# More copied groups, and single rows of table A fetched by SyncE, in a graph network layer on one Trainium2 core

## The chip, the cores and the metric

The kernel runs on one core of a Trainium2 chip. The time is the device time of the program in microseconds, as a median over runs. The engines are TensorE (PE in the profile, its weight loads PEld), VectorE (DVE), ScalarE (ACT), GpSimd (POOL) and SyncE (SP, which only issues transfers and loads registers).

## The reference

A graph network layer over 12,500 nodes of 64 features and 200,000 edges of 32 features, the edges sorted by destination. Everything is float32.

```python
msg_in = concatenate([nodes[row], nodes[col], edge_features], axis=-1)   # row = source, col = destination
messages = relu(msg_in @ mW1 + mb1) @ mW2 + mb2                          # hidden width 128
aggregated = segment_sum(messages, col, num_segments=12500)
upd_in = concatenate([nodes, aggregated], axis=-1)
x = layernorm(x + relu(upd_in @ uW1 + ub1) @ uW2 + ub2)
```

## The kernel before

The first layer's product is split in three: a node's share as a source is table A (`x @ mW1[:64]`, 12,500 rows of 128 floats in HBM), its share as a destination is table B, and the edge's own features are multiplied in place. Tables A and B are written by the kernel at the start.

The edges go in 1563 tiles of 128. Six tiles are a group, or step (`SUB`, 261 steps), two steps are a super (`SUP` = 12 tiles). For step `s`:

- `gather(s)` lets POOL issue one indirect transfer for each tile: 128 rows of table A, one for each edge's source, land in the `xg` buffer of the step (L220; the first ten steps gather rows of `x` instead). Nine buffers (`ROWB`) let POOL run ahead, and `frees` says after which step a buffer is free again.
- `windows(s + 2)` lets SP read the step's window numbers into registers (L285) and fetch 32 rows of table B for each tile or for several tiles with the same window (L293, later one transfer for each tile, L291).
- `select(g + 1)` (DVE, L254 and L260) compares destinations with window slots, and `load(g + 1)` (SP, L273) then fetches the edge features into the same operand; `loadd(g + 2)` (SP, L236) fetches destinations for the super after.
- `edge_part(s)` (PE, L384) multiplies the operand with the window rows and edge weights. `node_part(s)` adds the gathered rows (DVE, L410) and takes the relu (ACT, L411). `collect(s)` (PE, L443) sums the messages by destination.
- `update` and what follows it run once for some 400 nodes each and write the output (`store`, SP, L533).

In a *copied* group (`COPIED`) POOL gathers four tiles only. For the last two, x lies in SBUF column by column (`xtop`, `xbot`); the 128 columns of the edges' sources are copied one by one into `xc`, 64 by ACT (`singly`, L355) and 64 by DVE (`joined`, L362), from addresses that are loaded from `col_a` into registers, and PE multiplies `xc` with the weights (L387). The add is then L407 and the relu L408. `PACE` gives how many groups a step's copying advances, so how often a group is copied: 105 of 261.

The order of the program is written out by hand, step by step, and each engine runs its instructions in that order. Within step `s` SP has `windows(s + 2)`, in even steps `load(g + 1)`, in odd steps `loadd(g + 2)`, and now and then a store or a chunk of table B. A transfer of SP waits for the one that was issued eight before it.

Of the kernel before, what the change touches and what calls it, by code (L numbers as in the profile page):

```python
# [10 lines left out]
F32 = mybir.dt.float32  # L11
I32 = mybir.dt.int32
AF = mybir.ActivationFunctionType
ALU = mybir.AluOpType
AX = mybir.AxisListType
ET = mybir.EngineType

P = 128
N, D, DE, DH = 12500, 64, 32, 128
# [5 lines left out]
SUB = 6  # L25
# [4 lines left out]
NSUB = -(-NT // SUB)  # L30
# [39 lines left out]
XBASE = 8320  # L70
U8 = mybir.dt.uint8
YBASE = XBASE + 4 * XCOLS
LEAD = 8
PACE = ((11, 0.42), (50, 0.446), (130, 0.429), (261, 0))
FINAL = 258


# [5 lines left out]
COPIED = []  # L83
for s in range(NSUB):
    while progress(s) >= len(COPIED) + 1 and s + 3 < FINAL:
        COPIED.append(s + 3)
LAST = 4 * (N - 1)
ACTS, CHUNK = 64, 8

# [23 lines left out]
def gnn_kernel(ctx: ExitStack, tc: tile.TileContext, x1T, x, eT, e_rows, src, src_row, dst, dst_row, wlist, wrow, wnext, whalf,  # L113
# [24 lines left out]
    nc = tc.nc  # L138
# [4 lines left out]
    A = dram.tile([NPAD, DH], F32, name="tab_a")  # L143
# [11 lines left out]
    col_a = const.tile([P, 2, P, 2], I32, name="col_a")  # L155
# [47 lines left out]
    def tiles(s):  # L203
        return range(s * SUB, min((s + 1) * SUB, NT))

    def gathered_tiles(s):
        return tiles(s)[:SUB - 2 * (s in COPIED)]

    def gather(s):

# [14 lines left out]
    with tc.tile_pool(name="sup", bufs=2) as sup, tc.tile_pool(name="work", bufs=2) as work, tc.manual_schedule():  # L225
# [131 lines left out]
        def joined(s, part, of):  # L357

            todo = [(o, k, ACTS + e) for o, k, lo, hi in portion(s, P - ACTS) for e in range(lo, hi, 2)]
            for o, k, a, m in share(todo, part, of):  # L360
                for e, top, bot in addresses(k, a, m, ET.DVE):
                    nc.vector.tensor_tensor(o[:, e:e + 1].bitcast(I32), top.bitcast(I32), bot.bitcast(I32),  # L362
                                            op=ALU.bitwise_or)

        xc = {}

        def parts(n):

            if n == SUB:
                return [(slice(0, 2), SUB // 2)]  # L370
            return [(slice(b, b + 1), (n - b + 1) // 2) for b in range(2) if n > b]
# [18 lines left out]
        def node_part(s):  # L390

            n = len(tiles(s))
            pc = pcs.pop(s)
            h = work.tile([P, 2, SUB // 2, DH], F32, name="h")
            if s < XG:
                xt = xs.pop(s)
                for i in range(n):
                    k, b = divmod(i, 2)
                    q = 64 * b
                    nc.tensor.matmul(pc[:, b, k, :], xt[q:q + 64, k, :], w1a[q:q + 64], start=False,  # L400
                                     stop=i + 2 >= n)
                nc.scalar.activation(h, pc, AF.Relu)
            else:
                a = xg.pop(s)[0].rearrange("p (b k) f -> p b k f", b=2)
                if s in COPIED:
                    m = SUB // 2 - 1
                    nc.vector.tensor_tensor(pc[:, :, :m], pc[:, :, :m], a[:, :, :m], op=ALU.add)  # L407
                    nc.scalar.activation(h, pc, AF.Relu)  # L408
                for b, m in parts(n) if s not in COPIED else []:
                    nc.vector.tensor_tensor(h[:, b, :m], pc[:, b, :m], a[:, b, :m], op=ALU.add)  # L410
                    nc.scalar.activation(h[:, b, :m], h[:, b, :m], AF.Relu)  # L411
            hs[s] = h
# [270 lines left out]
        def rest(s):  # L683

            if 3 <= s < 9 and s % 2:
                others((s - 3) // 2 * 4, (s - 3) // 2 * 4 + 4)
            if 3 <= s < 11:
                zeros(s - 3, 8)
            if s == 6:
                first_nodes(8, NODES)  # L690
            if s == 9:
                columns_list()
            if s == 1:
                relative(8 * SUP, 8 * SUP + WCH)
            elif s == 2:
                relative(8 * SUP + WCH, NT)
                halves(4 * SUP, NTP // 2)
            elif s == BS:
                nc.sync.dma_start(wa, wrow.rearrange("o (p c) -> (o p) c", c=NSUP))
                nc.sync.dma_start(wb, wnext.rearrange("o (p c) -> (o p) c", c=NSUP))  # L700
                nc.scalar.dma_start(w2, mW2)
                nc.scalar.dma_start(u1a, uW1[D:2 * D, :])
                nc.scalar.dma_start(b2c, mb2.rearrange("(f o) -> f o", o=1))
                nc.vector.memset(uz[:D], 0.0)
                nc.vector.memset(ux[:D], 0.0)
                nc.vector.memset(eps, EPS)
                nc.vector.memset(ones, 1.0)
                nc.vector.tensor_copy(ux[D:], ident[D:, D:])
                nc.scalar.dma_start(uz[D:], uW1[0:D, :])
                nc.scalar.dma_start(ux[ONE:ONE + 1], ub2.rearrange("(o f) -> o f", o=1))  # L710
                nc.scalar.dma_start(ub1_s, ub1.rearrange("(f o) -> f o", o=1))
                nc.scalar.dma_start(u2, uW2)
            elif s == BS + 2:
                weights()
                checks()
# [54 lines left out]
        n = UPD[K - 1]  # L770
# [8 lines left out]
        for s in range(last + 2):  # L779
            g, j = divmod(s, SUP // SUB)  # L780
            while gathered < NSUB and frees(gathered) < s:
                gather(gathered)
                gathered += 1
            tail = due.get(s - 1) == K - 1

            def earlier(n):

                return next((u for d, u in due.items() if u + 2 < K and s - d == n and (n < 2 or u + 3 < K)), None)
            if tail:
                norm(K - 1)  # L790
            if s + 2 < NSUB:
                windows(s + 2)
            if s < NSUB:
                node_part(s)
                joined(s, 0, 3 if j == 0 and g + 1 < NSUP else 2)
            if s in at_end:
                for stage, u in at_end[s]:
                    stage(u)
            for stage, n in ((squares, 2), (statistics, 3), (deviation, 4)):
                if earlier(n) is not None:  # L800
                    stage(earlier(n))
            if 1 <= s <= NSUB:
                collect(s - 1)
            if s + 1 in due:
                close(due[s + 1])
            if j == 0 and g + 1 < NSUP:
                select(g + 1, s)
                load(g + 1)
                counts(g + 1)
            if j == 1 and g + 2 < NSUP:  # L810
                loadd(g + 2)
            if chunks and s >= BS and chunks[0] < NCH + NB * (s + 1 - BS) / (SUP // SUB * (GE - 1) - BS):
                chunk_b(chunks.pop(0), [Bv])
            if s in due and due[s] + 1 < K:
                carry(due[s] + 1)
            if s in due and due[s] + 2 != K:
                update(due[s])
            if s + 1 < NSUB:
                if s + 1 < XG:
                    transpose(s + 1)  # L820
                edge_part(s + 1)
            if earlier(4) is not None:
                norm(earlier(4))
            if earlier(1) is not None:
                residual(earlier(1))
            if s == UPD[K - 1]:
                update(K - 2)
            if s == UPD[K - 1] + 1:
                residual(K - 2)
            if due.get(s) == K - 1:  # L830
                activated(K - 1)
                residual(K - 1)
                squares(K - 1)
                statistics(K - 1)
                deviation(K - 1)
            if s + 2 in due and due[s + 2] + 1 < K:
                columns(due[s + 2])
            if s == UPD[K - 1]:
                columns(K - 1)
            rest(s)  # L840
            joined(s, 2 if j == 0 and g + 1 < NSUP else 1, 3 if j == 0 and g + 1 < NSUP else 2)
            singly(s, 0, 1)
            if s in due and due[s] + 2 < K:
                activated(due[s])
            if s == UPD[K - 1]:
                activated(K - 2)
            if tail:
                store(K - 1)
            if earlier(4) is not None:
                store(earlier(4))  # L850
# [3 lines left out]
                          skip_runtime_bounds_check_because="a count of edges")  # L854
    with tc.If(flag > 0), tc.tile_pool(name="gen", bufs=1) as up:
# [25 lines left out]
        first = up.tile([P, 1], F32, name="first")  # L881
        nc.vector.tensor_scalar(first, spare, -1.0, float(NPAD + P), op0=ALU.mult, op1=ALU.add)

        with tc.For_i(0, NT, 1) as t:
# [26 lines left out]
            pc = psum.tile([P, DH], F32, name="pcg", tag="pc")  # L911
# [4 lines left out]
            h = up.tile([P, DH], F32, name="hg")  # L916
# [6 lines left out]
            m = up.tile([P, 1], F32, name="m")  # L923
# [22 lines left out]
        with tc.For_i(0, NB, 1) as c:  # L946
# [24 lines left out]
            o = up.tile([P, D], F32, name="o")  # L971
# [49 lines left out]
```

## Time and profile before

| | |
|---|---|
| Time, median of 3 runs | 1716.34 us (1715.81 to 1716.83) |
| Profiled execution, its own time | 1714.18 us |
| Its span | 1712.3 us |
| Mean granted TensorE clock | 0.585 |
| Busy: PE, DVE, ACT, POOL | 1456.2, 1053.3, 1537.2, 1279.5 us |
| Bytes moved | 191.23 MB, 112 GB/s in the mean |

A line of a group gives the source line, the engine, the operation, the tiles written and read, the count, then the busy time in all, the nanoseconds of one, and the idle time of the engine just before them with what ended it. A line of the waits gives who waited for whom, the total in us, how often, and the longest. SP has no busy share: its instructions appear with their durations (least, median, most, in ns) where one source line is asked for, and its waits where they are asked for by engine. "issue" is idle time in which the engine waited for nothing that the profile shows.

### The profile page before, as it was taken

To read this page: it belongs to the slowest core of one execution; us is meant where nothing else is said; L and a number is where in the kernel's file an instruction comes from. 1 tells how busy PE (TensorE), PEld (TensorE's weight loads), DVE (VectorE), ACT (ScalarE), POOL (GpSimd) and SP (SyncE) were. 2 spreads that over 40 slices of the span, in tenths; PEclk is the share of its full clock that TensorE was granted. 3 is DMA by queue.
4 is the path that set the end of the run, shared out by engine and by line. 5 is a ranking of instruction groups with operands and counts; after the bars stand their busy time and mean duration, and the time that the engine had idled before them with its cause. 6 is when DMAs were issued, how large, how long until landed. Compare 5 with 4: busy or idle time off the path is not lost. (4 is left out here: it accounts for less than half of the span.)

```text
span 1712.3 us, 46949 instructions
## 1 busy us (share of the span) xinstructions
PE 1456.2 (85%) x9604; PEld 1251.9 (73%) x9604; DVE 1053.3 (62%) x7476; ACT 1537.2 (90%) x7151; POOL 1279.5 (75%) x1362
## 2 busy tenths in 40 slices
PE   2696889897888888898889999898878898999998
PEld 2585778776777786887777777776667677777776
DVE  1426666666666666666666666666666666666662
ACT  0277999999999999999999999999999999999982
POOL 7777777777777777777777777777777777777774
PEclk8675555555555555555555555556665656565666
DMA  8783434433333333333334343333333333443342
GB/s 209 207 180 100 119 109 127 117 104 89 98 93 101 95 100 97 99 103 100 104 101 110 106 113 103 106 110 103 106 103 109 111 107 108 113 112 105 105 113 76
DMA packets 205949, 191.23 MB, mean 112 GB/s; under 512 B 56129, under 2 KB 172053, under 8 KB 205669
## 3 DMA queue, kind: packets, MB, share of 16 engines
q1 hardware_dynamic: 147828, 92.48, 19.6%
q0 software_dynamic: 43296, 86.79, 18.6%
q10 hardware_dynamic: 14546, 8.93, 1.9%
q8 instruction: 91, 1.49, 0.4%
q14 instruction: 188, 1.54, 0.3%
HBM read 170.55 MB, written 17.50 MB: 110 GB/s over the span
## 5 line engine op out<-in xcount | busy, mean ns | idle before, releaser
L220 POOL DMA_INDIRECT xg<-tab_a,src_s x1293 | 1221.1, 944 | 394.2 <-issue 357.6
L355 ACT ACTIVATE xc<-xtop,xbot 128x1 f32 x6720 | 1274.5, 288 | 32.9 <-issue 22.9
L362 DVE TENSOR_TENSOR xc<-xtop,xbot 128x1 int32 x6720 | 575.0, 154 | 442.2 <-issue 429.5
L443 PE MATMUL sums<-sel,h 128*128 128x32 f32 x3126 | 643.3, 373 | 83.0 <-ACT h L408 42.5
L443 PEld LDWEIGHTS sums<-sel,h 128*128 128x128 f32 x3126 | 609.5, 296 | 108.0 <-ACT h L408 48.2
L384 PE MATMUL pc<-rhs,l 64*128 64x128 f32 x3126 | 418.7, 413 | 59.3 <-DMA l<-in_eT 15.2
L384 PEld LDWEIGHTS pc<-rhs,l 64*128 64x128 f32 x3126 | 348.8, 293 | 119.4 <-issue 62.8
L410 DVE TENSOR_TENSOR h<-pc,xg 128x768 f32<-128x768 f32 x147 | 139.5, 949 | 57.5 <-PE pc L384 27.8
L411 ACT ACTIVATE h<-h 128x768 f32<-128x768 f32 x147 | 122.3, 833 | 27.6 <-DVE h L410 26.8
L254 DVE TENSOR_TENSOR l<-l,cps 128x768 f32<-128x768 int32 (+1 forms) x134 | 126.7, 946 | 29.3 <-DMA l<-in_dst_row 17.4
L440 PEld LDWEIGHTS <-one 128*1 128x1 bf16 x1563 | 56.9, 83 | 89.3 <-issue 80.3
L440 PE MATMUL cnt<-sel,one 128*1 128x32 bf16 x1563 | 92.6, 187 | 0.5 <-issue 0.3
L408 ACT ACTIVATE h<-pc 128x768 f32<-128x768 f32 x105 | 83.8, 798 | 7.8 <-DVE pc L407 7.4
L407 DVE TENSOR_TENSOR pc<-pc,xg 128x512 f32<-128x512 f32 x105 | 73.4, 699 | 27.9 <-PE pc L387 23.8
L387 PE MATMUL pc<-w1a,xc 64*128 64x128 f32 x420 | 81.2, 388 | 0.0
L260 DVE TENSOR_TENSOR sel<-cps,drc 128x384 f32<-128x384 f32 x131 | 71.4, 545 | 12.0 <-PE sums L443 12.0
L387 PEld LDWEIGHTS pc<-w1a,xc 64*128 64x128 f32 x420 | 72.1, 301 | 0.0
L220 POOL DMA_INDIRECT xg<-in_x,src_s x60 | 57.4, 957 | 19.1 <-issue 17.7
L494 PE MATMUL cps<-ux,xw 128*128 128x64 f32 x252 | 45.9, 341 | 20.0 <-DVE sel L260 17.4
L480 PE MATMUL pu<-xw,uz 128*128 128x480 f32 (+1 forms) x64 | 61.2, 1059 | 0.0
L598 ACT COPY tb<-pb 128x512 f32<-128x512 f32 (+1 forms) x13 | 7.4, 570 | 58.7 <-DMA tab_a<-tb 26.8
L494 PEld LDWEIGHTS cps<-ux,xw 128*128 128x128 f32 x252 | 41.1, 247 | 25.4 <-DVE sel L260 19.6
(105 smaller groups left out, 691.6 us busy)
## 6 DMA issues: line engine op xcount, KB each, us to landing
l<-in_dst_row SPq DMA_DIRECT2D x262, 96.0 KB
l<-in_eT SPq DMA_DIRECT2D x262, 96.0 KB
xg<-tab_a,src_s POOLq DMA_INDIRECT x1293
rhs<-tab_b SPq DMA_DIRECT2D x361, 32.0 KB
tab_b<-tb SPq DMA_DIRECT2D x13, 512.0 KB
rhs<-tab_b SPq DMA_DIRECT2D x387, 16.0 KB
tab_a<-tb ACTq DMA_DIRECT2D x12, 512.0 KB
out<-y SPq DMA_DIRECT2D x31, 128.0 KB
```

Source lines behind the costliest of these rows:

```text
L220: nc.gpsimd.indirect_dma_start(out=a[:, i, :] if s < XG else a[:, i // 2, i % 2, :], out_offset=None, in_=A[:, :] if s >= XG else x[:, :], ...
L254: nc.vector.tensor_tensor(l[r], l[r].bitcast(I32), node[r].unsqueeze(2).broadcast_to([r.stop - r.start, SUP // 2, P]), op=ALU.is_equal)
L355: nc.scalar.activation(o[:, e:e + 1], top.bitcast(F32), AF.Identity, bias=bot.bitcast(F32))
L362: nc.vector.tensor_tensor(o[:, e:e + 1].bitcast(I32), top.bitcast(I32), bot.bitcast(I32), op=ALU.bitwise_or)
L384: nc.tensor.matmul(pc[:, b, k, :], L[g][q:q + 64, m, :], rhs[g % 2][q:q + 64, w, :], start=s >= XG or k == 0, stop=s >= XG and not copied)
L387: nc.tensor.matmul(pc[:, b, k, :], xc[s][q:q + 64], w1a[q:q + 64], start=False, stop=True)
L408: nc.scalar.activation(h, pc, AF.Relu)
L410: nc.vector.tensor_tensor(h[:, b, :m], pc[:, b, :m], a[:, b, :m], op=ALU.add)
L411: nc.scalar.activation(h[:, b, :m], h[:, b, :m], AF.Relu)
L440: nc.tensor.matmul(pn[:, bass.ds(ws[i], WIN)], one, SB[g][:, k0 + i, :, 1], start=False, stop=ends and i == n - 1)
L443: nc.tensor.matmul(ps[:, bass.ds(ws[i], WIN)], h[:, i % 2, i // 2, :], S[g][:, k0 + i, :], start=False, stop=ends and i == n - 1)
L494: nc.tensor.matmul(py[:, i], xw[u % 2][:, i * P:(i + 1) * P], ux, start=i == 0, stop=False)
```

## The change

`PACE` rises in its three stretches, so that 107 groups are copied. A second list, `SINGLE`, holds four groups (51, 97, 162 and 245) that are not copied, and in which POOL gathers four tiles only, too. The 256 rows of table A that the last two tiles need are fetched by SP, one row of 512 B in one transfer, into `xr`. `ROWPACE` gives the edges a step: 3.5 from step 12, 3.0 from 45, 2.3 from 90 and 1.6 from 136, two transfers an edge (one for each of the two tiles). `fetched(s)` issues a step's share at the end of the step: it loads the row numbers from `col_a` into SP's registers and issues the transfers. DVE then adds the gathered and the fetched rows in two instructions. `xr` has one buffer. In all there are 1024 such transfers in 204 steps, from step 12 to step 242.

```diff
-PACE = ((11, 0.42), (50, 0.446), (130, 0.429), (261, 0))
+PACE = ((11, 0.435), (50, 0.4565), (130, 0.4335), (261, 0))
...
+ROWPACE = ((12, 3.5), (45, 3.0), (90, 2.3), (136, 1.6))
+SINGLE, QUOTA = [], {}
+step, found = ROWPACE[0][0], 0.0
+while step < NSUB - 8:
+    done, a = 0, step
+    while done < P and step < NSUB - 8:
+        found += next(r for b, r in reversed(ROWPACE) if step >= b)
+        n = min(int(found) // 2 * 2, P - done)
+        found -= n
+        QUOTA[step] = len(SINGLE), done, done + n
+        done += n
+        step += 1
...
+    SINGLE.append(next(c for c in range(step + 1, NSUB) if c not in COPIED))
+    step = SINGLE[-1] + 1
...
-        return tiles(s)[:SUB - 2 * (s in COPIED)]
+        return tiles(s)[:SUB - 2 * (s in COPIED or s in SINGLE)]
...
+        A4 = A.rearrange("n (c d) -> (n c) d", c=4)
+
+        def fetched(s):
+
+            if s not in QUOTA or QUOTA[s][1] == QUOTA[s][2]:
+                return
+            i, lo, hi = QUOTA[s]
+            k = SINGLE[i] - LEAD
+            if lo == 0:
+                xr[SINGLE[i]] = work.tile([P, 2, DH], F32, name="xr", bufs=1)
+            o = xr[SINGLE[i]]
+            _, v = nc.values_load_multi_w_load_instructions(
+                col_a[k % P:k % P + 1, k // P].rearrange("k e b -> k (e b)")[:, 2 * lo:2 * hi], engines=[ET.SP], min_val=XBASE,
+                max_val=YBASE + LAST, skip_runtime_bounds_check_because="sources are node numbers")
+            for e in range(lo, hi):
+                for b, first in enumerate((XBASE, YBASE)):
+                    w = v[2 * (e - lo) + b].with_bounds(min_val=first, max_val=first + LAST, guaranteed_mod_val=0, out_of_modulus=4)
+                    nc.sync.dma_start(o[e:e + 1, b], A4[bass.ds(w - first, 4), :].rearrange("c d -> (c d)").unsqueeze(0))
...
+                if s in SINGLE:
+                    m = SUB // 2 - 1
+                    nc.vector.tensor_tensor(h[:, :, :m], pc[:, :, :m], a[:, :, :m], op=ALU.add)
+                    nc.vector.tensor_tensor(h[:, :, m], pc[:, :, m], xr[s], op=ALU.add)
+                    nc.scalar.activation(h, h, AF.Relu)
...
             rest(s)
+            fetched(s)
             joined(s, 2 if j == 0 and g + 1 < NSUP else 1, 3 if j == 0 and g + 1 < NSUP else 2)
             singly(s, 0, 1)
```

More of the change, by code (lines that the diff above doesn't have):

```diff
@@ L86 @@
         COPIED.append(s + 3)
+ROWPACE = ((12, 3.5), (45, 3.0), (90, 2.3), (136, 1.6))
[10 more added lines that the diff above has]
+        step += 1
+    if done < P:
+        QUOTA = {k: v for k, v in QUOTA.items() if k < a}
+        break
+    SINGLE.append(next(c for c in range(step + 1, NSUB) if c not in COPIED))
+    step = SINGLE[-1] + 1
 LAST = 4 * (N - 1)
@@ L365, in gnn_kernel @@
         xc = {}
+        A4 = A.rearrange("n (c d) -> (n c) d", c=4)
[14 more added lines that the diff above has]
+                    nc.sync.dma_start(o[e:e + 1, b], A4[bass.ds(w - first, 4), :].rearrange("c d -> (c d)").unsqueeze(0))
+        xr = {}
         def parts(n):
@@ L408, in node_part @@
                     nc.scalar.activation(h, pc, AF.Relu)
-                for b, m in parts(n) if s not in COPIED else []:
+                if s in SINGLE:
[3 more added lines that the diff above has]
+                    nc.scalar.activation(h, h, AF.Relu)
+                for b, m in parts(n) if s not in COPIED and s not in SINGLE else []:
                     nc.vector.tensor_tensor(h[:, b, :m], pc[:, b, :m], a[:, b, :m], op=ALU.add)
```

## The prediction

> **What bounds the kernel now.** I read the page first (busy time of the engines, then the costliest groups), then busy time by stretch, then SyncE's own waits by stretch, and last what one of its transfers costs to issue.
>
> ```profile
> PE 1456.2 (85%) x9604; PEld 1251.9 (73%) x9604; DVE 1053.3 (62%) x7476; ACT 1537.2 (90%) x7151; POOL 1279.5 (75%) x1362
> ...
> L220 POOL DMA_INDIRECT xg<-tab_a,src_s x1293 | 1221.1, 944 | 394.2 <-issue 357.6
> L355 ACT ACTIVATE xc<-xtop,xbot 128x1 f32 x6720 | 1274.5, 288 | 32.9 <-issue 22.9
> L362 DVE TENSOR_TENSOR xc<-xtop,xbot 128x1 int32 x6720 | 575.0, 154 | 442.2 <-issue 429.5
> ```
>
> POOL looks 75% busy, but its idle time is "issue": it waits for nothing that the profile shows. One gather costs (1221.1 + 394.2)/1293 = 1.249 us, and 1353 of them (60 more at the start) fill the program. One copied column costs ACT (1274.5 + 32.9)/6720 = 0.195 us and DVE (575.0 + 442.2)/6720 = 0.151 us.
>
> ```profile
> core 0: us, PE busy (x) PEld busy (x) DVE busy (x) ACT busy (x) POOL busy (x), PEclk, DMA share, GB/s
> 141.00:344.00 203.00, 169.55 (x1177) 154.97 (x1177) 136.24 (x941) 187.61 (x900) 153.61 (x163) 0.53 0.41 114
> 344.00:623.00 279.00, 236.07 (x1524) 208.44 (x1526) 180.77 (x1385) 276.20 (x1337) 210.89 (x224) 0.54 0.34 96
> 623.00:907.00 284.00, 247.11 (x1564) 215.55 (x1560) 186.26 (x1413) 281.27 (x1365) 214.66 (x228) 0.54 0.36 101
> ...
> 1072.00:1339.00 267.00, 225.66 (x1485) 189.87 (x1484) 170.85 (x1249) 254.20 (x1205) 201.74 (x214) 0.60 0.38 107
> ...
> 1590.00:1712.30 122.30, 108.49 (x707) 87.35 (x706) 60.74 (x349) 79.22 (x340) 78.34 (x83) 0.65 0.35 97
> ```
>
> The stretches are the change's own: counted by the adds of L407 and L410 (one a step from step 10), 141 us is about step 13, 344 step 45, 623 step 90, 907 step 136, 1072 step 163, 1339 step 204 and 1590 step 243. From 344 to 907 ACT is busy 276.2 of 279 and 281.3 of 284 us: there the consumers of the gathers (PE, DVE, ACT) run behind POOL at ACT's pace and catch up. From 1072 on ACT has 5% to spare, and POOL sets the pace, about 6.4 us a step. So two engines are full in turn; the third, SyncE (SP), is on no busy line, and it is the one that the change loads. Its waits, in six stretches from 141, 344, 623, 907, 1072 and 1339 us in this order:
>
> ```profile
> SPq L273 <- DVE l L254: 106.9, 16, 21.1
> SPq L608 <- DVE tb L606: 26.7, 10, 5.9
> ...
> SPq L273 <- DVE l L254: 139.1, 22, 8.9
> SPq L533 <- DVE y L526: 5.5, 3, 3.6
> ...
> SPq L273 <- DVE l L254: 94.5, 22, 7.2
> SPq L533 <- DVE y L526: 6.9, 4, 3.1
> ...
> SPq L273 <- DVE l L254: 30.9, 14, 6.0
> ...
> SPq L533 <- DVE y L526: 4.2, 3, 1.9
> ...
> SPq L273 <- DVE l L254: 50.9, 19, 6.1
> ...
> SPq L533 <- DVE y L526: 2.3, 2, 1.2
> ...
> SPq L273 <- DVE l L254: 26.6, 18, 2.7
> SPq L291 <- PE pc L384: 6.3, 23, 0.4
> SPq L533 <- DVE y L526: 3.3, 5, 0.8
> SPq L291 <- PE cps L496: 2.4, 6, 0.9
> ```
>
> That is SP's free time: 134, 145, 101, 35, 53 and 30 us. It shrinks because the rows of table B come in more and more transfers (L293, then L291). I leave the short waits on PE out of it, because their releases fall within the issue of the transfer before; the last stretch has some 9 us of them in the rows shown. In its last stretch SP is free 30 of 251 us:
>
> ```profile
> 1402.23 3.93 SPq L291 DMA_DIRECT2D rhs<-tab_b  x6
> 1406.27 0.83 SPq L273 DMA_DIRECT2D l<-in_eT  x2
> 1408.12 3.09 SPq L291 DMA_DIRECT2D rhs<-tab_b  x6
> ```
>
> Six issues take 3.09 us from the first start to the last end, one after the other.
>
> **The change, part by part.** *POOL.* 105 copied groups become 107 (two gathers less each), and four groups lose two gathers each: 1353 become 1341, 12 x 1.249 = 15.0 us less, spread over the program.
>
> *ACT, DVE, PE.* Two more copied groups are 128 more columns on ACT and on DVE: 128 x 0.195 = 24.9 us and 128 x 0.151 = 19.4 us. Where ACT is full (steps 45 to 135) the rate rises by 0.015 to step 50, by 0.0105 to step 130 and by 0.0045 after, in groups of 64 ACT columns each: 61 columns, 61 x 0.195 = 12 us on the path there, 6 of them from step 90 on; before 344 us ACT has 15 us of room and after 1072 us 5%, so the rest I cost at nothing while that room lasts (13 us if it does not). PE's eight more matmuls and the second DVE add of the four groups are some 4 us in all, beside ACT's work.
>
> *SP.* 256 single rows for each of four groups: 1024 transfers, each with a register instruction, and 204 register loads. Between the stretches' borders fall 228, 260, 200, 80, 128 and 128 transfers and 33, 43, 44, 20, 32 and 32 loads. The trace has no transfer of one table row; its neighbours are:
>
> ```profile
> L291 SPq FUSED_REGOPS  x387: 37/37/43, 1271.0 to 1688.1; - x194
> ...
> L291 SPq MOVE rhs<-tab_b x387: 29/29/35, 1271.1 to 1688.2; - x194
> L291 SPq DMA_DIRECT2D rhs<-tab_b x387: 296/316/1555, 1271.2 to 1688.3; - x194
> ...
> L311 SPq DMA_DIRECT2D cols<-in_src_row x2: 275/357/439, 111.3 to 113.9; - x2
> ...
> L285 SPq TENSOR_LOAD <-wint x245: 447/720/1219, 35.5 to 1686.0; - x123
> ...
> L608 SPq DMA_DIRECT2D tab_b<-tb x14: 398/405/581, 26.2 to 354.8; - x14
> ...
> L655 SPq DMA_DIRECT2D wint<-in_wlist x1: 313/313/313, 13.7 to 13.7; - x1
> ```
>
> L291 is the same thing with 32 rows of 512 B: 316 ns, with 37 + 29 ns of register work before it. Six of them in 3.09 us are (3.09 - 0.316)/5 = 0.555 us each, of which 0.04 is a wait instruction that a fetch lacks: 0.51 us at the upper end. The lower end is the same without the transfer's own 0.316: 0.20 us. What one row costs between them is the disputed number. One row of 8 KB cost 313 ns (L655), as much as 32; but of L311's two transfers, alike but for 128 and 124 rows, the second took 275 instead of 439 ns, 0.63 times, and a count that can't be dealt out evenly is what a single row has too. I take 0.63 x 0.316 = 0.20, so 0.40 us a fetch, and 0.72 + 0.05 = 0.77 us a load (L285's median; 0.447 at the least).
>
> [...]
>
> SP's added work against its free time, at 0.40 and 0.77: 91 + 25 = 116 against 134; 104 + 33 = 137 against 145; 80 + 34 = 114 against 101; 32 + 15 = 47 against 35; 51 + 25 = 76 against 53; and 76 against 30. The first two fit. The third is over by 13, of which ACT's 6 us lengthen the steps anyway: 7. Then 12, 23 and 46. SP issues in order: behind each run of fetches stand the next windows (L291, L293) and the eT loads (L273), and PE waits for those.
>
> ```profile
> PE pc L384 <- DMA l<-in_eT: 15.2, 17, 1.8
> ```
>
> PE already waits for eT 17 times, so there is little lead to eat: one step, 6 us. After step 242 the fetches end; the last stretch held 122 us at POOL's pace with PE busy 108.5, so 14 us can be made up there. POOL's 15 us are then worth nothing: it runs ahead until its nine buffers are full.
>
> The added waits are cheap. DVE's second add waits for the group's last fetch, issued two or three steps earlier; a new group's first fetch waits for that add, one step behind it.
>
> Sum: 12 (ACT) + 7 + 12 + 23 + 46 = 100; less 6 and 14: **80 us slower**. The profiled execution took 1714.2 us, 1.9 above its span and 2.2 below the median of the runs: 1794 us, 1795 on the scale of the runs.
>
> **The rivals.** *A dearer fetch*, the same way: at 0.51 us (L291 whole) the six stretches are over by 7, 21, 29, 21, 37 and 60, 175 in all, less 20: 1869 us. For it: L655. *A cheaper one*, 0.30: ACT 12, then 4, 10 and 33, 59 less 20: 1753 us.
>
> *The fetches are hidden, and POOL's cut counts.* This is the other side. The last stretch decides: at 0.20 us a fetch and 0.52 a load (L285's least) its need is 128 x 0.20 + 32 x 0.52 = 42 us, just what its 30 us and the short waits on PE (12 with the rows not shown) hold. Then SP is never late, ACT's 12 us are made up after 1072 us, and the end comes with POOL's: 1714.2 - 15.0 = 1699 us. It decides below about 0.22 us. For it: L311's shorter issue, and rates of fetching that fall as SP's free time falls. Against it: the register work alone is 0.20.
>
> *They cancel.* Between 0.22 and 0.27 us the last stretch's overrun of 10 to 20 us eats the 15: 1711 to 1718 us, no change.
>
> *ACT becomes the bound* without SP being late: 24.9 us more on an engine busy 90%. Its room after 1072 us (267 - 254 us in one stretch alone) takes that up; it would end at 1699 to 1705 us, and counts with the second rival.
>
> **How the numbers follow.** About 0.2% (3.4 us) is what a measurement tells from no change. Slower by SP: 0.72, of which some 0.40 lie from 0.30 to 0.45 us a fetch, the rest on both sides. Hidden: 0.22. Cancelled: 0.06. The likeliest case alone spans 1735 to 1870 us. The range has to hold the hidden case as well, so 1697 to 1880 us; about 0.1 lies above (a fetch beyond 0.52 us) and a little below.
>
> **What would show it.** Right: SP's wait L273 <- DVE L254 nearly gone from 623 us on; PE's waits for eT and for the rows of table B (L384) grown to tens of microseconds from about 907 us; ACT below 95% there; POOL with gaps that end with a consumer's add and not with "issue"; the fetch line at some 0.40 us from start to start. Wrong: fetches at 0.25 us or less from start to start, SP still waiting for DVE after 1339 us, POOL unbroken to the end and a span near 1697 us. If SP is saturated from the first stretch on, the fetch is dearer than I took it.

## The result, and the profile after

| | before | after |
|---|---|---|
| Time, median of 6 runs each | 1716.59 us (1715.81 to 1717.89) | 1872.89 us (1868.43 to 1879.98) |
| Profiled execution and its span | 1714.18, 1712.3 us | 1879.98, 1878.1 us |
| Mean granted clock | 0.585 | 0.561 |

The change makes the kernel slower by 156 us: 1.0915 times (95% interval 1.0891 to 1.094). The forecast was 80 us slower. The sign and the mechanism held, the size did not.

In the kernel after, lines have moved: the gathers are L238 (before L220), ACT's copies L373 (L355), DVE's L380 (L362), the edge products L422 (L384), the adds L445 and L453 (L407 and L410), SP's eT load L291 (L273), the load of destinations L254 (L236), the select L272 (L254), the rows of table B L311 and L309 (L293 and L291), their register load L303 (L285). New are the fetch L401 and its register load L395. The page of the kernel after:

```profile
span 1878.1 us, 50490 instructions
PE 1525.9 (81%) x9612; PEld 1311.8 (70%) x9612; DVE 1069.7 (57%) x7608; ACT 1574.1 (84%) x7279; POOL 1268.8 (68%) x1350
...
L238 POOL DMA_INDIRECT xg<-tab_a,src_s x1281 | 1210.2, 945 | 533.7 <-issue 345.6
L373 ACT ACTIVATE xc<-xtop,xbot 128x1 f32 x6848 | 1298.3, 281 | 54.2 <-issue 42.5
L380 DVE TENSOR_TENSOR xc<-xtop,xbot 128x1 int32 x6848 | 585.1, 155 | 476.1 <-issue 466.5
...
L422 PE MATMUL pc<-rhs,l 64*128 64x128 f32 x3126 | 456.2, 428 | 224.9 <-DMA l<-in_eT 125.8
...
L272 DVE TENSOR_TENSOR l<-l,cps 128x768 f32<-128x768 int32 (+1 forms) x134 | 127.4, 951 | 179.4 <-DMA l<-in_dst_row 171.7
...
xr<-tab_a SPq DMA_DIRECT2D x1024, 0.5 KB
```

No engine with a busy line is full: every share went down, and POOL's gathers now have 188 us of idle time that is not "issue" (533.7 - 345.6), where before it was 37 (394.2 - 357.6). The waits of the kernel after (who waited for whom, us in total, times, longest) name what they wait for:

```profile
DVE l L272 <- DMA l<-in_dst_row: 171.7, 68, 6.8
POOL xg L238 <- DVE h L453: 126.5, 71, 5.9
PE pc L422 <- DMA l<-in_eT: 125.8, 55, 5.0
...
POOL xg L238 <- DVE pc L445: 38.1, 23, 4.5
...
PE pc L422 <- DMA rhs<-tab_b: 27.2, 29, 2.6
```

DVE and PE wait for transfers that SP issues (destinations, edge features, rows of table B), and POOL waits for the consumers' adds to free its buffers: 126.5 + 38.1 = 165 us, close to the 166 us by which the span grew. SP's wait for the select in the same six stretches as before (steps 13 to 45, 45 to 90, 90 to 136, 136 to 163, 163 to 204, 204 to 243; the last has none, and its longest wait is shown instead):

```profile
SPq L291 <- DVE l L272: 16.1, 5, 13.8
...
SPq L291 <- DVE l L272: 9.0, 1, 9.0
...
SPq L291 <- DVE l L272: 7.0, 4, 5.1
...
SPq L291 <- DVE l L272: 1.3, 3, 0.6
...
SPq L291 <- DVE l L272: 5.4, 3, 3.3
...
SPq L309 <- PE pc L422: 6.6, 18, 1.4
```

Before, these were 106.9, 139.1, 94.5, 30.9, 50.9 and 26.6 us. All of SP's free time can be added up from its records in the trace, as every gap of over 0.15 us between two of its instructions, less 0.05 us. By that it had 134, 143, 109, 36, 55 and 32 us free in the six stretches before, and has 26, 12, 10, 3, 8 and 4 us after: next to none, almost from the first stretch on. Busy time by stretch, in the kernel after, with borders at about the same steps:

```profile
core 0: us, PE busy (x) PEld busy (x) DVE busy (x) ACT busy (x) POOL busy (x), PEclk, DMA share, GB/s
141.00:358.00 217.00, 174.81 (x1163) 159.75 (x1163) 140.72 (x983) 196.57 (x943) 164.19 (x174) 0.51 0.41 111
358.00:651.00 293.00, 232.55 (x1512) 207.70 (x1512) 185.49 (x1410) 282.70 (x1363) 215.25 (x228) 0.54 0.35 93
651.00:961.00 310.00, 253.28 (x1568) 220.70 (x1568) 189.84 (x1448) 290.99 (x1398) 220.88 (x234) 0.53 0.36 95
...
1445.00:1750.00 305.00, 257.73 (x1458) 212.07 (x1460) 163.86 (x1192) 247.55 (x1155) 186.15 (x198) 0.56 0.34 89
1750.00:1878.00 128.00, 108.99 (x725) 87.33 (x723) 63.93 (x376) 84.05 (x364) 47.93 (x51) 0.67 0.31 82
```

ACT, at 99% from step 45 to 135 before, is at 96 and 94% (282.70 of 293, 290.99 of 310), and 81% in the last fetched stretch. What one fetch costs SP, by source line and by the timeline (start, length, issues in the run):

```profile
L401 SPq FUSED_REGOPS  x1024: 46/46/61, 141.4 to 1762.8; - x171
L401 SPq MOVE xr<-tab_a x1024: 29/29/39, 141.5 to 1762.9; - x171
L401 SPq DMA_DIRECT2D xr<-tab_a x1024: 220/228/734, 141.6 to 1762.9; - x171
...
L395 SPq TENSOR_LOAD <-col_a x204: 490/512/1096, 140.9 to 1760.8; - x102
```

```profile
217.35 3.22 SPq L401 DMA_DIRECT2D xr<-tab_a  x8
...
1501.75 3.57 SPq L309 DMA_DIRECT2D rhs<-tab_b  x6
1505.42 2.28 SPq L291 DMA_DIRECT2D l<-in_eT  x2
1508.47 1.57 SPq L401 DMA_DIRECT2D xr<-tab_a  x4
1511.39 3.08 SPq L309 DMA_DIRECT2D rhs<-tab_b  x6
```

Eight fetches in 3.22 us are (3.22 - 0.23)/7 = 0.43 us from start to start. In the second piece, SP goes from one block of issues to the next; the gaps of 0.8 and 1.4 us hold the register loads. Between step 13 and step 243 the blocks of fetches took 581 us: 454.4 for the fetches and 126.4 for their register loads (worked out from the trace's SP records, as are all sums of SP's time below).

### The profile page after: what moved, and what is told of

It is laid out like the page before. It is cut to its first block, busy times and chain, and to the rows that moved or that the text cites. A ratio compares the mean times of both kernels' runs of the same rounds, so it can differ in the third digit from the quotient of the medians.

```text
span 1878.1 us, 50490 instructions
## 1 busy us (share of the span) xinstructions
PE 1525.9 (81%) x9612; PEld 1311.8 (70%) x9612; DVE 1069.7 (57%) x7608; ACT 1574.1 (84%) x7279; POOL 1268.8 (68%) x1350
## 5 line engine op out<-in xcount | busy, mean ns | idle before, releaser
L238 POOL DMA_INDIRECT xg<-tab_a,src_s x1281 | 1210.2, 945 | 533.7 <-issue 345.6
L373 ACT ACTIVATE xc<-xtop,xbot 128x1 f32 x6848 | 1298.3, 281 | 54.2 <-issue 42.5
L380 DVE TENSOR_TENSOR xc<-xtop,xbot 128x1 int32 x6848 | 585.1, 155 | 476.1 <-issue 466.5
L486 PE MATMUL sums<-sel,h 128*128 128x32 f32 x3126 | 660.2, 379 | 21.0 <-ACT h L454 14.2
L486 PEld LDWEIGHTS sums<-sel,h 128*128 128x128 f32 x3126 | 626.2, 303 | 41.3 <-ACT h L454 15.9
L422 PE MATMUL pc<-rhs,l 64*128 64x128 f32 x3126 | 456.2, 428 | 224.9 <-DMA l<-in_eT 125.8
L422 PEld LDWEIGHTS pc<-rhs,l 64*128 64x128 f32 x3126 | 375.2, 302 | 296.8 <-issue 202.7
L272 DVE TENSOR_TENSOR l<-l,cps 128x768 f32<-128x768 int32 (+1 forms) x134 | 127.4, 951 | 179.4 <-DMA l<-in_dst_row 171.7
L453 DVE TENSOR_TENSOR h<-pc,xg 128x768 f32<-128x768 f32 x141 | 133.7, 949 | 35.5 <-PE pc L422 18.3
L445 DVE TENSOR_TENSOR pc<-pc,xg 128x512 f32<-128x512 f32 x107 | 74.8, 699 | 19.7 <-PE pc L425 13.4
L537 PE MATMUL cps<-ux,xw 128*128 128x64 f32 x252 | 55.9, 395 | 34.7 <-DVE sel L278 33.3
L537 PEld LDWEIGHTS cps<-ux,xw 128*128 128x128 f32 x252 | 50.6, 297 | 42.0 <-DVE sel L278 37.0
L278 DVE TENSOR_TENSOR sel<-cps,drc 128x384 f32<-128x384 f32 x131 | 71.8, 548 | 13.6 <-PE sums L486 13.3
L238 POOL DMA_INDIRECT xg<-in_x,src_s x60 | 57.6, 960 | 19.2 <-issue 18.0
```

What stands on the lines that cost most here:

```text
L238: nc.gpsimd.indirect_dma_start(out=a[:, i, :] if s < XG else a[:, i // 2, i % 2, :], out_offset=None, in_=A[:, :] if s >= XG else x[:, :], ...
L272: nc.vector.tensor_tensor(l[r], l[r].bitcast(I32), node[r].unsqueeze(2).broadcast_to([r.stop - r.start, SUP // 2, P]), op=ALU.is_equal)
L373: nc.scalar.activation(o[:, e:e + 1], top.bitcast(F32), AF.Identity, bias=bot.bitcast(F32))
L422: nc.tensor.matmul(pc[:, b, k, :], L[g][q:q + 64, m, :], rhs[g % 2][q:q + 64, w, :], start=s >= XG or k == 0, stop=s >= XG and not copied)
L486: nc.tensor.matmul(ps[:, bass.ds(ws[i], WIN)], h[:, i % 2, i // 2, :], S[g][:, k0 + i, :], start=False, stop=ends and i == n - 1)
L537: nc.tensor.matmul(py[:, i], xw[u % 2][:, i * P:(i + 1) * P], ux, start=i == 0, stop=False)
```

## The experiments

The disputed points: is it SP's time, the bytes and rows in flight, the order in which SP issues, or the raised copy rates? All ratios are to the kernel before as it was timed beside each run (medians of 1714.53 to 1716.92 us), with a 95% interval.

| kernel | median us | ratio |
|---|---|---|
| rates alone | 1725.01 | 1.0058 (1.0039 to 1.0076) |
| rows alone | 1868.74 | 1.0886 (1.0859 to 1.0913) |
| transfers left out | 1723.47 | 1.0057 (1.0036 to 1.0078) |
| register loads as filler | 1723.83 | 1.0063 (1.0038 to 1.0087) |
| empty instructions as filler | 1843.97 | 1.0743 (1.0725 to 1.076) |
| rows of 32 B | 1879.73 | 1.0945 (1.0914 to 1.0976) |
| half the rows | 1775.53 | 1.0355 (1.0329 to 1.0381) |
| two groups, gentle | 1711.40 | 0.997 (0.9958 to 0.9982) |
| two groups at the full rates | 1725.98 | 1.0071 (1.0055 to 1.0087) |
| destinations one super earlier | 1865.04 | 1.0877 (1.0859 to 1.0895) |
| fetches first | 1882.46 | 1.097 (1.095 to 1.0991) |
| two groups, in between | 1711.03 | 0.9983 (0.997 to 0.9997) |

One more difference has no experiment of its own. The granted TensorE clock is 0.561 after and 0.585 before, and PE is busy 70 us longer. Between steps 13 and 243 SP is free for only 63 of 1613 us, which leaves little for a slower PE to add there; and of the four executions of the rows alone the fastest (1861.91 us) had the lowest clock (0.560).

**The raised rates alone** (no single groups).

```diff
-while step < NSUB - 8:
+while False and step < NSUB - 8:
```

> Leaves out the fetched rows (no single groups) and keeps the raised rates: 107 copied groups, 1349 gathers. SP-time theory (the changed kernel is slow because SyncE has more to issue than time): SP is as before, so no slower than before; POOL has 4 gathers of 1.249 us less, 1711 to 1717 us. Rival 'copies' (the 128 more columns on ACT and DVE are what costs): 25 us of ACT and more, 1735 us or above, most of the 156 us. Rival 'traffic' (the fetched rows delay other transfers): as before, 1711 to 1717.

It cost 10 us where no loss was expected. In a window after step 163 ACT, which before had 254.2 us of work in 267, has 260.66 (busy time by stretch of this kernel):

```profile
1072.00:1339.00 267.00, 223.50 (x1519) 189.26 (x1526) 172.98 (x1280) 260.66 (x1242) 201.76 (x215) 0.62 0.41 107
```

By step 136 it had lost 23 us and by step 260 won back 9 of them. ACT's room after 1072 us did not repay the earlier loss in full.

**The rows alone** (rates as before; the groups fall on 51, 97, 161 and 243).

```diff
-PACE = ((11, 0.435), (50, 0.4565), (130, 0.4335), (261, 0))
+PACE = ((11, 0.42), (50, 0.446), (130, 0.429), (261, 0))
```

> Keeps the fetched rows in four groups (51, 97, 161, 243) and puts the old rates back: 105 copied groups. SP-time theory: 1024 fetches and 204 loads are all there, 1850 to 1880 us. Rival 'copies': 1705 to 1720 us. Rival 'traffic': 1850 to 1880.

154 us of the 156 remain, so by the medians the two costs hardly add, which fits columns of ACT that lie beside a full SP. The intervals are some 4 us either way, so a part of the rates' 10 us may still lie in the 156.

**The transfers left out, and SP's time put back.** The first kernel leaves the 1024 transfers out; the register loads, now unused, left the program as well, so SP has no more to issue than before; the buffer of the rows is set to zero instead. The second was to fill SP's time with register loads; nobody reads them, and they turned into empty instructions of 0.058 us, so SP was hardly loaded (it still waits 419.6 us for the select, 468.0 before) and this run decides nothing. The third uses those empty instructions on purpose, 7 for each transfer and 9 for each load.

```diff
-            for e in range(lo, hi):
-                for b, first in enumerate((XBASE, YBASE)):
-                    ...
-                    nc.sync.dma_start(o[e:e + 1, b], ...)
+            # first kernel: nothing; second: 3 * (hi - lo) // 2 register loads
+            for e in range(14 * (hi - lo) + 9):   # third kernel
+                nc.values_load_multi_w_load_instructions(...)
```

> Leaves out the 1024 transfers; the last two tiles of the four groups get zeros instead of table rows. The 204 register loads, the raised rates and the missing gathers stay. SP-time theory: SP has 204 x 0.57 = 116 us more instead of 546, within its free time in each stretch (18 of some 30 us in the last), and POOL has 12 gathers less: 1700 to 1712 us. Rival 'traffic': the same. Rival 'copies': 1735 us or above.

> Leaves out the 1024 transfers as the run before, and gives SP register loads of four words in their place, three for every four transfers (0.56 us against 4 x 0.42 = 1.68 us for three): the same SyncE time, no data. SP-time theory: as slow as the changed kernel, 1845 to 1895 us. Rival 'traffic' (the rows on their way delay the edge features and window rows): 1700 to 1715 us.

> As the run with loads only (no transfer, zeros in their place), and SyncE gets empty instructions of 0.058 us each in the places of the fetches: seven for each transfer (0.41 us; the transfer took 0.42) and nine for each register load (0.53 us). The same SyncE time as the changed kernel, nothing moved. SP-time theory: as slow as the changed kernel, 1850 to 1885 us. Rival 'traffic' (rows on their way, and eight transfers in flight at most, delay the others): 1715 to 1730 us, as the run with the raised rates alone.

Without the transfers the kernel is back at the time of the raised rates (1723.47 and 1725.01), above the 1700 to 1712 us expected, so POOL's eight further gathers less bring nothing there. With 544 us of empty instructions and no transfer at all, 127 of the 156 us return, with the same waits; 1850 to 1885 us had been expected. From SP's own waits in that kernel, whole run (468.0 us for the same wait before, 59.0 after):

```profile
SPq L291 <- DVE l L272: 66.3, 31, 13.8
```

From the waits of its other engines (the edge products are L423 there):

```profile
DVE l L272 <- DMA l<-in_dst_row: 144.9, 66, 7.1
PE pc L423 <- DMA l<-in_eT: 94.5, 51, 4.2
```

So most of the loss comes back by SP's time alone. For the other 29 us no run gives the cause by itself, but this kernel has 66 us less of SP's time between steps 13 and 243 than the changed one: 36 less in the blocks, and 30 less in SP's other rows, for a reason that was not foreseen. The register load for the windows (720 ns in the median before), by its source line in the kernel after:

```profile
L303 SPq TENSOR_LOAD <-wint x245: 466/862/1238, 35.1 to 1857.1; - x123
```

With rows of 32 B (below):

```profile
L303 SPq TENSOR_LOAD <-wint x245: 466/819/1232, 36.2 to 1852.7; - x123
```

With empty instructions:

```profile
L303 SPq TENSOR_LOAD <-wint x245: 431/717/1216, 35.1 to 1814.5; - x123
```

By these medians it is longer by 0.14 us in the kernel after. The mean over the 221 loads of steps 13 to 243 tells the sum better: 0.743 us before, 0.827 after, 0.824 with rows of 32 B and 0.721 with empty instructions. Between the last kernel and the one after that is 24 of those 30 us, so the transfers cost SP time beyond their own issue.

**Rows of 32 B** instead of 512 B.

```diff
-                    nc.sync.dma_start(o[e:e + 1, b], A4[bass.ds(w - first, 4), :].rearrange("c d -> (c d)").unsqueeze(0))
+                    nc.sync.dma_start(o[e:e + 1, b, :8], A4[bass.ds(w - first, 1), :8])
```

> The same 1024 transfers with 32 B instead of 512 B each (the rest of the last two tiles' rows is left at zero). SP-time theory: the issue costs the same, 1860 to 1885 us. Rival 'traffic by bytes': 1715 to 1740 us. Traffic by count of transfers alone would leave it at 1860 to 1885 too.

No better than 512 B (its interval overlaps the changed kernel's): bytes in flight are not the cause.

**Half the rows**, and as many register loads.

```diff
-                for b, first in enumerate((XBASE, YBASE)):
+                for b, first in enumerate((XBASE,)):
```

> Fetches only the first of the two tiles' rows in each single group (512 transfers; the second tile gets zeros). SP-time theory: SyncE has 512 x 0.42 + 204 x 0.57 = 331 us more instead of 546; by stretches 68, 80, 67, 28, 45, 45 against 134, 145, 101, 35, 53, 30 us of free time, over by 15 us in the last alone: 1725.0 of the raised rates + 15 + up to 10 for free time that can't be used, 1735 to 1755 us. If each fetch costs a fixed delay whatever SP's free time, half of the 148 us that the fetches cost beside the raised rates: near 1799 us.

59 us remain, 20 more than the upper end expected; 10 of them are the raised rates' own. SP then has 180 us free between steps 13 and 243, most of it in waits for the select (from SP's waits in this kernel, whole run):

```profile
SPq L291 <- DVE l L272: 163.2, 74, 16.3
```

Most of these 180 us, 159, lie before step 136, where little more is lost than by the rates alone. But time is lost before a stretch's free time is used up, too: in steps 136 to 163 the blocks take 32 of the 36 us that were free before, and in steps 163 to 204 48 of 55 (SP's other rows grow there by 1 and 6 us). These stretches lose 8 and 13 us more than with the rates alone, while 4.5 and 13.5 us of SP's time stay free.

**Two rivals on the order.** The first lets the load of destinations (for which DVE waits 171.7 us) be issued one super earlier, with a fourth operand buffer and one buffer less for POOL; the second puts a step's fetches ahead of the wait for the select.

```diff
-            if j == 1 and g + 2 < NSUP:
-                loadd(g + 2)
+            if j == 1 and g + 3 < NSUP:
+                loadd(g + 3)
```

```diff
+            fetched(s)          # at the step's start
...
-            fetched(s)          # after rest(s)
```

> The changed kernel with the destination rows (in_dst_row) fetched one super earlier, into a fourth operand buffer; for the room of it POOL has eight row buffers instead of nine. SyncE issues the same instructions. SP-time theory: VectorE's 172 us of waits for the destination rows go, but SyncE's time is the same; at most its 63 us of unused time are won: 1815 to 1870 us. Rival 'latency' (a late fetch of the destination rows holds the chain, not SyncE's time in all): back to 1725 to 1760 us.

> The changed kernel with a step's fetches issued ahead of the wait for the comparison (in even steps between the window rows and the edge features), instead of at the end of the step. The same SyncE work. SP-time theory: within 15 us of the changed kernel, 1858 to 1888 us. If the place of the fetches in the order decides: a change of more than 30 us, either way.

The first won 6 us (150 over the kernel before on its chip, where the changed kernel has 156). The wait for destinations, 171.7 us in the changed kernel, is no longer among the largest, and the one for edge features has grown from 125.8 us (from the waits of that kernel):

```profile
PE pc L422 <- DMA l<-in_eT: 170.4, 72, 4.8
```

So in these two kernels a full SP is felt as a late load: with that one gone the next one is late. The second cost 11 us more. SP's work was not quite the same there: the fetches' register loads took 819 ns in the median instead of 512, and the blocks 46 us more in all, while SP's other rows took 24 us less. Neither order decides.

**Two groups, three rates of fetching**, all with the copy rates of before. At the rates of the change (groups 51 and 97, done at step 95), gentle (73 and 215), and in between (62 and 129, done at step 127):

```diff
-ROWPACE = ((12, 3.5), (45, 3.0), (90, 2.3), (136, 1.6))
+ROWPACE = ((12, 2.3), (45, 2.0), (90, 1.2), (136, 0.5))   # gentle
+ROWPACE = ((12, 2.7), (45, 2.5), (90, 1.6), (136, 0.5))   # in between
...
-while step < NSUB - 8:
+while step < NSUB - 8 and len(SINGLE) < 2:                # all three
```

> Old rates (105 copied groups) and only the first two single groups (51, 97) at the full rates of the change, so SyncE is loaded like the changed kernel up to step 95 and like the kernel before after it. In the run with the rows and the old rates the steps were 29 us behind at step 90. SP-time theory: about 35 us behind near step 96, a part of it made up where the kernel before waited for POOL (steps 136 on), POOL's 4 gathers less: 1725 to 1745 us. If lateness is never made good: 1750 us. If the first two stretches had the room that the prediction gave them: 1709 to 1717 us.

> Old rates (105 copied groups) and only two single groups (73 and 215) at 2.3, 2.0, 1.2 and 0.5 edges a step: about 60% of SyncE's free time in each stretch up to step 213. SP-time theory: SP stays free enough, and POOL has 4 gathers less, where it sets the pace: 1709 to 1717 us. If any fetch ahead of the window and feature loads costs time: 1725 us or above.

> As the gentle run (old rates, two single groups, now 62 and 129) with 2.7, 2.5 and 1.6 edges a step, all fetched by step 127: about 100 of 134, 115 of 145 and 85 of 106 us of SyncE's free time in the first three stretches, none after. SP-time theory with free time usable to three quarters: 1710 to 1720 us, some microseconds behind by step 128 and made up after. If it is usable in full: 1707 to 1713 us, as the gentle run. If only to 60%: 1720 us or above.

At the full rates it lost 24.5 us by step 90, shortly before the fetches end, and won 14 back after step 136 with SP free; by the medians it is 11 us slower. The gentle one is 0.3% faster than the kernel before. From its page and its SP waits:

```profile
L238 POOL DMA_INDIRECT xg<-tab_a,src_s x1289 | 1219.8, 946 | 392.9 <-issue 361.8
```

```profile
SPq L291 <- DVE l L272: 182.8, 96, 15.5
```

Four gathers less at 1.249 us are 5.0 us; the medians differ by 5.5 (0.3% of 1716.9). The one in between gains 4.0 us; its time lies in two of the ranges expected, so it does not tell free time that is usable in full from free time that is usable to three quarters. The gains fit the view that a gather less counts where SP keeps free time and ACT gets no more columns, but no run leaves out the gathers alone. The gentle version beats both kernels, the one in between by an interval that all but reaches 1.

## Why the prediction was right in its mechanism and wrong in its size

Time added in each stretch, against the kernel before, with the border at the first product (L422) of a step. The added time up to step 13 is 4.9 us, and after step 260 it is -3.5; the sum is the 166 us by which the spans differ. Each column is one execution: the rates alone and the transfers left out, which load SP nearly alike, differ by 3.4 us before step 13 and by up to 2.7 us in a stretch.

| steps | forecast | after | rates alone | half the rows | two groups full | in between |
|---|---|---|---|---|---|---|
| 13 to 45 | 0 | 12.0 | 4.5 | 5.6 | 7.3 | 4.1 |
| 45 to 90 | 6 (ACT) | 17.0 | 7.4 | 3.7 | 17.0 | 7.0 |
| 90 to 136 | 13 | 26.0 | 5.9 | 10.5 | 0.1 | -0.3 |
| 136 to 163 | 12 | 21.2 | -6.3 | 1.5 | -7.5 | -8.0 |
| 163 to 204 | 23 | 32.6 | -1.0 | 12.0 | -1.3 | -2.4 |
| 204 to 243 | 46 | 50.2 | -3.1 | 26.4 | -1.6 | -4.0 |
| 243 to 260 | -14 | 5.5 | 1.0 | 0.2 | -1.2 | 1.4 |

*The price of SP's work: right in the sum, in part by luck.* 0.40 us a fetch and 0.77 a load were taken; the runs show 0.43, and 0.512 + 0.05 = 0.57 for the load. Over the six stretches that made 566 us, and 581 were measured: the fetches took 454 us where 410 were reckoned and the loads 126 where 157 were, two misses that nearly cancel. One row was indeed cheaper to issue than 32 (228 against 316 ns), less so than L311's 0.63 times suggested; what made the second of L311's two transfers shorter, no run shows. A row of 32 B took the same 228 ns as one of 512 B. The rival "A dearer fetch" gives nearly the measured time (1869 us), but with 0.51 us: its number is met and its cause is not.

*The mechanism: right.* SP has next to no free time left, PE waits for eT (125.8 us, half of it before step 136 already) and table B (27.2), ACT is below 95% from step 90 on, POOL's gaps end with a consumer's add. That DVE would wait still longer for destinations (171.7), which also stand behind the fetches, the prediction did not name. Its test "if SP is saturated from the first stretch on, the fetch is dearer" misled: SP was all but saturated there (26 of 221 us free), with a fetch dearer by 0.03 to 0.05 us only.

*The step that failed is the free time.* The prediction let a stretch cost only what exceeds its free time ("The first two fit", then 7, 12, 23 and 46). Every stretch lost more, 4 to 13 us, 59 in all. In SP's records: the blocks took 581 us, SP's other rows grew by 23 (946 to 969; 19 of it is the longer register load L303), and its free time shrank by 445 only, from 508 to 63. So 581 + 23 - 445 = 159 us of added time, the sum of the six stretches. The terms mis-sized there are, against a forecast of 94 us from SP (13 + 12 + 23 + 46): blocks 15 more than taken, other rows 23 more, 37 more of the free time not used (63 against the 18 + 8 us that the first two stretches were to leave), and, on the gain side, 10 us more free time before than the prediction's rows of waits gave (508 against 498): 94 + 15 + 23 + 37 - 10 = 159. The stretches of the kernel with half the rows that were filled to about 90%, and that lost 8 and 13 us with time left, show as well that free time was not used to the end. Why it was not is argued, not shown: SP issues in order (in the timeline above its blocks follow one another), and a block put in front of the next load makes that load late even if SP is free later in the same step.

*"14 us can be made up" after step 242: wrong*, 5.5 us were lost. The 14 us were read from POOL and PE, not from SP. In SP's records it has work for 95 of the 108 us between steps 243 and 260 before, 106 of 114 after; so it had little room to catch up in.

*The lead of 6 us: not seen.* The two ends outside the stretches come to +1.4 us.

*ACT's 12 us: right alone, not in the sum.* The rates alone lose 13.3 us in steps 45 to 135, and 9.8 before. Of the latter 5.3 fall before step 13, where the transfers left out lose 1.9 at the same rates, so ACT's 15 us of room held in the main and little of the "13 if it does not" is seen. ACT's 5% to spare from 1072 us on was read from one stretch; from 1339 us on it was 3% (242.52 of 251 us). But beside a full SP they hardly count by the medians: 156 with them, 154 without.

*POOL's cut worth nothing: right for this kernel*, and the gentle run fits its full worth of 1.249 us a gather elsewhere. "The fetches are hidden" is so for two groups at 2.3, 2.0, 1.2 and 0.5 edges a step; at the change's rates even half the transfers were not hidden. (The 0.52 us a load taken there is not quite L285's least, 0.447 + 0.05 = 0.50 us; that moves its need by less than 1 us.)

## What to carry to other kernels

An engine that only issues transfers and loads registers, as SP does here, has no busy line in these pages; add up its free time by stretch, and price the added instructions by what each occupies it. Do not plan to use that free time up. Here the blocks took 92% of the first stretch's free time (123 of 134 us), and 12.0 us were lost there, 7.3 with two groups and the old rates. The one in between took 74, 86 and 68% in the first three stretches and lost 4.1 and 7.0 us and won 0.3; the gentle one took 64, 70 and 61% and lost 1.9, 0.4 and 4.2 us, the last of which it made good in the next stretch (6.5 us won). And time lost to such an engine was made up later only where that same engine had room (with two groups at the full rates 14 us after step 136; in the changed kernel, with SP busy for 106 of the last 114 us before step 260, 5.5 us more were lost), so the end of the program has to be looked up for it too.

## What the runs showed that was not expected

- A transfer of one row holds SP for 228 ns in the median, whether 32 or 512 B (248 ns where half the rows are fetched); with its two register instructions it takes 0.43 us from start to start in the kernel after. 1024 of them move only 0.5 MB and cost 154 us (rows alone).
- SP's register load for the windows takes 862 instead of 720 ns in the median where all the single rows are fetched, and 0.08 us longer in the mean, with 512 B as with 32 B; with 544 us of empty instructions it does not (717 ns). What in the transfers lengthens it stays open.
- The copy rates, raised by 1 to 4%, cost 10 us by themselves, although ACT is busy only 90% of the span.
